# A hybrid of deformable convolution, attention and experts on one core: batch 0's samples by TensorE, sums sent by ScalarE, values copied by VectorE, fewer transfers of features, and one finishing job at a time in its heavy part

## The chip, the cores and the metric

The kernel runs on one core of a Trainium2 chip. The metric is the device time of one execution in microseconds. A core has five engines, each with an instruction order of its own: TensorE (PE in the profile; its weight loads are shown as PEld), VectorE (DVE), ScalarE (ACT), GpSimd (POOL) and SyncE (SP). "SPq", "ACTq" and "POOLq" are the same sequencers issuing transfers. Matmul results go to PSUM banks, from which VectorE or ScalarE copies them.

## The reference

The input x is [4, 128, 64, 64] in float32; a batch has 4096 positions, called tokens from the second layer on.

```python
# layer 0
g = groupnorm(x, 32 groups)
offset, mask = conv3x3(g), sigmoid(conv3x3(g))         # 18 and 9 channels
samples = bilinear_sample(g, grid + offset) * mask     # 9 taps of 128 channels a position
x = x + einsum("bckhw,ock->bohw", samples, w_flat) + bias
# layer 1, t = tokens of x, [4, 4096, 128]
n = layernorm(t)
c = cos(n.reshape(16 heads of 8) + theta)
q = [prod(c[1:]), c0*c1, c0*c1*c2, ...]                # 8 features of a head; q = k = v
ctx = softmax(q q^T / sqrt(8)) q                       # 4096 x 4096 for each head
x1 = layernorm(n + ctx @ w_comb.T + b_comb)
zf = cos(x1[..., :8]) * cos(ry)
t = t + layernorm(x1 + relu(zf @ w1.T + b1) @ w2.T + b2)
t = t + top2_of_8_experts(layernorm(t))                # router softmax, 8 matrices of 128 x 128
```

## The kernel before

A batch is cut into 8 chunks of 512 tokens, and the 16 heads into 4 groups of 4. The unit of attention is a step: for one run (a batch, a head group, a chunk of queries) and one tile of 128 keys, TensorE makes four score matmuls (L1261) into two PSUM tiles `sc`, ScalarE takes two exponentials of 128x1024 (L1270), and TensorE adds four context matmuls (L1281) to `acc`. There are 3700 steps. Where a chunk's exponentials are the mirror of a later one's, a few of them are turned by VectorE (`st`), sent to DRAM (`etd`) and read back (`et`) instead of being computed twice.

The order of TensorE, VectorE, SyncE and GpSimd is written out by hand: the main loop (from L1400 on) issues one step after another, and between steps a planner (`Beside`) places fills, pieces of the other work. The pieces come from Python generators that yield `need(pe, dve, lat, hold, after)`, an estimate of the piece's time; `Beside` keeps a planned clock that moves by 1.82 a step, a credit of TensorE time, and a list of things to do `later`, among them most transfers. Three kinds of job are queued:

- "prepare", for one batch: GroupNorm, a table of corner values in DRAM, offsets, then `deform`, which gathers samples, `convolved` (the conv of a chunk, the residual, the tokens) and `features`. Where a step needs a chunk that isn't there, the planner forces prepare work in front of it.
- "finish", for each chunk whose 4 head groups are done (`park_context`): `finish` loads the context, makes the reciprocals of the softmax sums and takes them through DRAM to spread them, then goes through `attention_out` (ao_ps), `feed_forward` (z_ps, h_ps, f_ps) and `experts` (u_ps, l_ps, e_ps, y_ps), and sends the output. At most two of the generators `finishing` are active at once, and each takes one chunk after another.
- "turned", for the mirrored exponentials.

After the last step `beside.drain()` writes out what finishing is left.

Batch 0 has nothing to hide its preparation behind, so its first 26 runs (steps 0 to 159, `opening`) work with the chunks that are there: chunk 1 is first needed at step 16, chunk 2 at 64, chunk 3 at 104, chunks 4 to 7 between 256 and 292. Such a run ends with a partial sum: ScalarE copies `acc` to `cu` (L1491), SyncE sends it to `part` (L1126) and loads it back for the run that goes on with it (L1456). Batch 1 begins at step 964, batch 2 at 1876, batch 3 at 2788; in batch 3 one chunk after another is done, the last with step 3700.

`deform` handles a chunk in 12 units of 128 positions by three taps: three indirect gathers on GpSimd (L625), a multiplication by the corner weights and two sums on VectorE (L645, L650, L651). For batch 0's chunks 0 and 1 the samples are then transposed on TensorE (L662) into PSUM and copied by VectorE into the tile `sT` of the conv. All other chunks use three VectorE transposes a unit (L686), four transfers to DRAM (`smd<-tr`, L698) and four back (`sT<-smd`) for each three taps of a chunk. Gathers run up to four units ahead for batch 0's first 36 units and two ahead otherwise.

`features` ends in `rn`: GpSimd copies it to `fx` (L823), four transfers write that to `fqd` (L827), TensorE transposes it (fT_ps, L836), VectorE splits the result into a high and a low part, and eight transfers (L846, L847) write each part twice to `kTd` (rows for keys) and twice to `qTd` (rows for queries).

Of the kernel before, what the change touches and what calls it, by code (L numbers as in the profile page):

```python
# [224 lines left out]
def kernel(  # L225
# [373 lines left out]
    def deform(b, tab, idx, wt, rest):  # L599
# [7 lines left out]

        def early(n):

            return b == 0 and n < 3 * 12  # L610

        def gather(last):

# [20 lines left out]
        for n, (ch, kg, j) in enumerate(units):  # L634
            progress[b] = 0.1 + 0.9 * n / len(units)
            if b == 0 and n == 36:
                yield need(dve=5.0)
                settle()
            while not ahead:
                yield need(lat=0.5)  # L640
            v, landed = ahead.pop(0)
            v4 = v.rearrange("p k (q c) -> p (k q) c", c=C)
            w12 = wt[:, j, 3 * kg : 3 * kg + 3, :].rearrange("p k q -> p (k q)")
            yield need(dve=ve(1536), after=landed)
            nc.vector.tensor_tensor(v4, v4, w12[:, :, None].to_broadcast([P, 12, C]), ALU.mult)  # L645
            if moved:
                yield need(pe=0.01, dve=ve(384))
                moved.pop()()
            yield need(dve=ve(768) + ve(384))
            nc.vector.tensor_tensor(v[:, :, : 2 * C], v[:, :, : 2 * C], v[:, :, 2 * C :], ALU.add)  # L650
            nc.vector.tensor_tensor(v[:, :, :C], v[:, :, :C], v[:, :, C : 2 * C], ALU.add)  # L651
            if b == 0 and ch < 2:


                if n % 12 == 0:
                    while len(summed) < ch:
                        yield need(lat=0.5)
                    sT = big.tile([P, KK, CH], F32, tag="xs", name=f"sT_first{ch}")
                yield need(pe=tr(3), lat=FREE, hold=True)
                pt = misc(f"sT_ps{j}_{kg}")  # L660
                for k in range(3):
                    nc.tensor.transpose(pt[:, P * k : P * (k + 1)], v[:, k, :C], ident)  # L662

                def move(sT=sT, kg=kg, i=j % 4, pt=pt):
                    nc.vector.tensor_copy(
                        sT[:, 3 * kg : 3 * kg + 3, P * i : P * (i + 1)],
                        pt[:, : 3 * P].rearrange("p (k c) -> p k c", c=P),
                    )

                moved.append(move)  # L670
                beside.later(beside.now + 0.8, lambda n=n: gather(n))
                if n % 12 == 11:
                    yield need(pe=0.01, dve=ve(384))
                    moved.pop()()
                    featuring.append(True)
                    beside.add("prepare", convolved(b, ch, sT), 0.5, True)
                    if ch == 0:
                        yield from rest
                continue

            yield need(dve=ve(384))
            if j % 4 == 0:
                beside.flush(sent)
                tr9 = work.tile([P, 4, 4, 4, 32], F32, tag="st", name=f"tr{b}_{ch}_{kg}", bufs=NST)
            for k in range(3):
                nc.vector.transpose(  # L686
                    out=tr9[:, k, :, j % 4, :],
                    in_=v[:, k, :C].rearrange("p (c i) -> p c i", i=32),
                )
            beside.later(beside.dve, lambda n=n: gather(n))  # L690
            if j % 4 < 3:
                continue
            while kg == 0 and len(featuring) > 1:
                yield need(lat=1.0)

            def put(ch=ch, kg=kg, tr9=tr9):
                for o in range(4):
                    nc.sync.dma_start(  # L698
                        out=smd[ch % 2][:, 3 * kg : 3 * kg + 3, :, o].rearrange(
                            "i k c n -> i (k c) n"  # L700
                        ),
                        in_=tr9[32 * o : 32 * (o + 1), :3].rearrange("p k c j t -> p (k c) (j t)"),
                    )

            sent = beside.dve
            beside.later(sent, put)
            if kg == 2:

                while len(summed) < ch if b == 0 else featuring:
                    yield need(lat=1.0)  # L710
                featuring.append(True)
                beside.later(
                    beside.dve + 0.1,
                    lambda ch=ch: beside.add("prepare", convolved(b, ch), 0.5, True),
                )
# [77 lines left out]
    def features(b, ch, x2, mean, rstd):  # L793

        yield from layer_norm_stats(x2, mean, rstd, "lt")

        def temp(name, shape=(P, 4 * C), dt=F32):
            return work.tile(list(shape), dt, tag="p2", name=f"{name}{b}_{ch}", bufs=NP2)

        fx, f4 = fxs[ch % NFX]  # L800
        xt, a, n, r = temp("xt"), temp("ra"), temp("rn"), temp("rr")
        yield need(dve=ve(128, 4))
        normalized(xt.rearrange("p (i c) -> p i c", c=C), x2, mean, rstd)
        beside.later(
            beside.dve,
            lambda: nc.sync.dma_start(out=xtd[b][ch].rearrange("p i c -> p (i c)"), in_=xt),
        )
        yield need(dve=ve(512, 2))
        a8 = a.rearrange("p (h d) -> p h d", d=HD)
        x8 = xt.rearrange("p (h d) -> p h d", d=HD)  # L810
        nc.vector.tensor_tensor(a8, x8, rx_sb[:, None, :].to_broadcast([P, 64, HD]), ALU.add)
        yield from cosine(a, a, n, r, ve(512))
        c8 = a.rearrange("p (j h d) -> p j h d", j=4, d=HD)
        q8 = n.rearrange("p (j h d) -> p j h d", j=4, d=HD)
        yield need(dve=ve(64, 7))
        nc.vector.tensor_tensor(q8[:, :, :, 0], c8[:, :, :, 1], c8[:, :, :, 2], ALU.mult)
        for d in range(3, HD):
            nc.vector.tensor_tensor(q8[:, :, :, 0], q8[:, :, :, 0], c8[:, :, :, d], ALU.mult)
        yield need(dve=ve(64, 7), lat=0.2)
        nc.vector.tensor_tensor(q8[:, :, :, 1], c8[:, :, :, 0], c8[:, :, :, 1], ALU.mult)  # L820
        for d in range(2, HD):
            nc.vector.tensor_tensor(q8[:, :, :, d], q8[:, :, :, d - 1], c8[:, :, :, d], ALU.mult)  # L822
        beside.later(beside.dve, lambda: nc.gpsimd.tensor_copy(f4[:, :, :, :HD], q8))  # L823

        def put_values():
            for g in range(NGRP):
                nc.sync.dma_start(out=fqd[b % 2][ch][g], in_=fx[:, :, QG * g : QG * g + QL])  # L827

        beside.later(beside.dve + 2.0, put_values)

        yield need(pe=tr(4), dve=ve(512, 2))
        pt = misc(f"fT_ps{b}_{ch}")
        for i in range(4):
            nc.tensor.transpose(pt[:, P * i : P * (i + 1)], n[:, P * i : P * (i + 1)], ident)  # L836
        hi, lo = temp("hiT"), temp("loT")
        nc.vector.tensor_copy(hi.bitcast(F32R), pt)
        nc.vector.tensor_tensor(lo.bitcast(F32R), pt, hi, ALU.subtract)

        def put(part, fT):

            kd = kTd[b % 2][ch].rearrange("(h l r d) n -> l r h d n", l=2, r=2, d=HD)
            qd = qTd[b % 2][ch].rearrange("(h r l d) n -> l r h d n", l=2, r=2, d=HD)
            for rep in range(2):
                nc.sync.dma_start(out=kd[part, rep], in_=fT)  # L846
                nc.sync.dma_start(out=qd[part, rep], in_=fT)  # L847

        beside.later(beside.dve - ve(512), lambda: put(0, hi))
        beside.later(beside.dve, lambda: put(1, lo))  # L850
        prepared[b, ch] = beside.dve + 9.0
        featuring.pop(0)

# [230 lines left out]
    def finish(b, ch):  # L1084
# [19 lines left out]
            in_=rdd[b][ch].rearrange("h q n -> h (q n)")[:, None, :].to_broadcast([HEADS, HD, CH]),  # L1104
        )
        yield from attention_out(b, ch, r, aT, a4)
        yield from feed_forward(b, ch, x4, a4)
        yield from experts(b, ch, x4)


    def park_context(b, g, sc, cu):
# [8 lines left out]

        beside.later(beside.dve, put)

    def park_sums(g, sc, cu, when):

        def put():
            nc.sync.dma_start(out=partd[g][sc], in_=cu)  # L1126
            storing.discard((g, sc))

        storing.add((g, sc))
        beside.later(when, put)  # L1130

# [90 lines left out]

    landing = {}
    fetched = {}
    groups, done, active = {}, [], []

    def finishing():

# [179 lines left out]
    with tc.manual_schedule(engines={PE, DVE, SP, POOL}):  # L1410
# [6 lines left out]
        while n < len(steps):  # L1417
# [71 lines left out]
                cu = work.tile([P, 512], F32, tag="cu", name=f"cu{run}", bufs=NCU)  # L1489
            if by_act:  # L1490
                nc.scalar.copy(cu, acc)  # L1491
            elif kind in (WHOLE, FIRST):
                nc.vector.tensor_copy(cu, acc)  # L1493
            else:
                nc.vector.tensor_tensor(cu, cu, acc, ALU.add)
            if kind in (WHOLE, LAST):
                park_context(b, g, sc, cu)
            else:
                park_sums(g, sc, cu, beside.now + 3.0 if by_act else beside.dve)
        alone.append(True)  # L1500
        beside.drain()

# [72 lines left out]
```

## Time and profile before

| | |
|---|---|
| median of 11 runs | 7461.57 us (7446.05 to 7471.73) |
| the profiled execution's own time | 7456.55 us |
| its span | 7454.8 us |
| ScalarE busy | 6853.9 us, of it 6839.9 in the 7400 exponentials |
| PE busy | 7028.4 us |
| VectorE busy | 4464.6 us |
| POOL busy | 1657.5 us |
| first exponential of the attention starts | 174.7 us |
| last exponential ends | 7370.9 us |

A line of the costliest groups reads: source line, engine, operation, output<-input, shapes, count | busy us, mean ns of one | idle us of the engine just before them, and what ended most of it. A line of the waits reads: engine, tile and line that waited <- who released it: us in total, times, longest us. The table of stretches gives, for start:end, the length and for each engine the busy us, then the granted TensorE clock as a share of full speed, the DMA engines' share and GB/s. A line of the timeline reads: start us, duration us, engine, line, operation, tile, count [idle us of the engine before it <- what ended it].

### The profile page before, as it was taken

The page shows a single profiled execution, that of the slowest core. Times are in us where ns is not written, and L with a number is a line of the kernel's source. Part 1 is how long each engine was busy: PE and PEld are TensorE (multiplying, and loading weights), DVE is VectorE, ACT ScalarE, POOL GpSimd, SP SyncE. Part 2 cuts the span into 40 slices and gives each one's busy share as a digit, 9 for nine tenths or more (in the row PEclk, how much of TensorE's full clock was granted, in tenths as well). Part 3 has the DMA queues.
Part 4 walks back from the last instruction along what each step waited for, and adds up shares of the span by engine and source line. Part 5 has one row for each costly group of instructions (what it writes and reads, how often), then busy time and mean ns, then how long its engine had stood idle before and what let it go on. Part 6 is the DMA issues. An engine that isn't in the chain of part 4 may idle for free.

```text
span 7454.8 us, 180754 instructions
## 1 busy us (share of the span) xinstructions
PE 7028.4 (94%) x73848; PEld 2360.6 (32%) x73848; DVE 4464.6 (60%) x8950; ACT 6853.9 (92%) x7467; POOL 1657.5 (22%) x1326
## 2 busy tenths in 40 slices
PE   3689999899999999999999999999999999999997
PEld 2222232223333333333333333323333333333333
DVE  7756366676445787875544778875444554455544
ACT  0579999899999999999999999989999999999995
POOL 5545034443001433431000434430000000000000
PEclk6889999999999999999999999999999999999998
DMA  6777567988446988887555888996454466666651
GB/s 182 223 210 230 139 233 241 304 257 289 152 162 229 297 261 273 288 277 235 201 180 193 268 287 293 315 313 226 172 180 150 158 233 232 239 223 229 231 196 64
DMA packets 909789, 1689.53 MB, mean 227 GB/s; under 512 B 150754, under 2 KB 384124, under 8 KB 858268
## 3 DMA queue, kind: packets, MB, share of 16 engines
q1 hardware_dynamic: 809102, 1371.37, 55.3%
q0 software_dynamic: 92160, 302.06, 12.5%
q8 instruction: 580, 9.50, 0.5%
q10 hardware_dynamic: 7694, 4.52, 0.2%
q14 instruction: 253, 2.07, 0.1%
HBM read 1027.51 MB, written 650.14 MB: 225 GB/s over the span
## 4 chain that ended last, share of the span: by engine, by line
PE 81%; DMA 9%; DVE 4%; SPq 1%; issue 1%; ACT 1%; POOL 0%; POOLq 0%; DVEq 0%; ACTq 0%
PE acc L1281 39%; PE sc L1261 23%; PE acc L1214 5%; PE conv_ps L281 4%; PE e_ps L281 4%; DMA et<-etd 3%; PE f_ps L281 2%; DMA etd<-st 1%; DMA sT<-smd 1%; PE om_ps L533 1%; DMA v<-tab,idx 1%; DMA smd<-tr 1%; ACT e L1270 1%; DVE v L645 1%; PE ao_ps L281 0%
## 5 line engine op out<-in xcount | busy, mean ns | idle before, releaser
L1270 ACT ACTIVATE e<-sc 128x1024 f32<-128x1024 f32 x7400 | 6839.9, 1084 | 411.3 <-PE sc L1261 332.4
L1281 PE MATMUL acc<-e,qf 128*9 128x512 f32 (+1 forms) x29600 | 3904.9, 600 | 11.3 <-ACT cu L1491 6.2
L1261 PE MATMUL sc<-qT,kT 32*128 32x512 f32 x14800 | 2326.1, 499 | 108.1 <-ACT e L1270 56.2
L1261 PEld LDWEIGHTS sc<-qT,kT 32*128 32x128 f32 x14800 | 929.2, 183 | 3528.3 <-ACT e L1270 3330.4
L625 POOL DMA_INDIRECT v<-tab,idx x1152 | 1457.4, 1265 | 1496.8 <-DVE tr L686 869.3
L1140 DVE STREAM_TRANSPOSE st<-e 128x1024 f32<-128x1024 f32 x792 | 937.1, 1221 | 709.1 <-ACT e L1270 586.3
L1281 PEld LDWEIGHTS acc<-e,qf 128*9 128x9 f32 (+1 forms) x29600 | 681.1, 92 | 577.7 <-issue 316.5
L396 POOL TENSOR_TENSOR r<-ln_t,expo 128x4 f32<-128x4 f32 x96 | 112.2, 1169 | 3095.7 <-DVE ln_t L394 3048.3
L645 DVE TENSOR_TENSOR v<-v,wt 128x1536 f32<-128x1536 f32 x384 | 667.0, 1737 | 126.1 <-DMA v<-tab,idx 123.7
L1214 PE MATMUL acc<-et,qv 128*9 128x128 f32 x12672 | 503.5, 277 | 65.6 <-DMA et<-etd 65.6
L1065 DVE TENSOR_TENSOR eo<-e_ps,gt 128x512 f32<-128x512 f32 x256 | 175.2, 686 | 536.6 <-PE e_ps L281 532.9
L650 DVE TENSOR_TENSOR v<-v 128x768 f32<-128x768 f32 x384 | 367.1, 956 | 10.1
L281 PE MATMUL conv_ps<-sT,wconv_sb 128*32 128x256 f32 x4320 | 351.0, 399 | 14.9 <-DMA sT<-smd 14.8
L1214 PEld LDWEIGHTS acc<-et,qv 128*9 128x9 f32 x12672 | 270.0, 91 | 264.5 <-issue 201.8
L686 DVE STREAM_TRANSPOSE tr<-v 128x128 f32<-128x128 f32 x1080 | 249.4, 282 | 49.1 <-DMA etd<-st 40.4
L1493 DVE COPY cu<-acc 128x512 f32<-128x512 f32 x116 | 80.2, 691 | 282.6 <-PE acc L1281 280.7
L651 DVE TENSOR_TENSOR v<-v 128x384 f32<-128x384 f32 x384 | 215.8, 562 | 13.3
L396 POOL TENSOR_TENSOR rstd<-lt_t,expo 128x4 f32<-128x4 f32 x32 | 56.5, 1766 | 545.2 <-DVE lt_t L394 509.6
L281 PE MATMUL f_ps<-w_sb,h 128*32 128x128 f32 x4096 | 164.8, 280 | 0.0
L950 DVE TENSOR_SCALAR h<-h_ps,b_sb 128x512 f32<-128x512 f32 x128 | 94.9, 743 | 99.5 <-PE h_ps L948 89.7
L823 POOL COPY fx<-rn 128x512 f32<-128x512 f32 x32 | 26.9, 839 | 522.5 <-DVE rn L822 319.1
L965 DVE TENSOR_TENSOR a<-a,f_ps 128x512 f32<-128x512 f32 x32 | 21.9, 686 | 195.7 <-PE f_ps L281 195.7
(227 smaller groups left out, 3164.5 us busy)
## 6 DMA issues: line engine op xcount, KB each, us to landing
etd<-st SPq DMA_DIRECT2D x396, 1024.0 KB
et<-etd SPq DMA_DIRECT2D x396, 1024.0 KB
kT<-kTd SPq DMA_DIRECT2D x372, 256.0 KB
smd<-tr SPq DMA_DIRECT2D x360, 192.0 KB
sT<-smd SPq DMA_DIRECT2D x360, 192.0 KB
qT<-qTd SPq DMA_DIRECT2D x166, 256.0 KB
atd<-cu SPq DMA_DIRECT2D x128, 256.0 KB
qf<-fqd SPq DMA_DIRECT2D x372, 72.0 KB
```

Source lines behind the costliest of these rows:

```text
L281: nc.tensor.matmul(dst[c : c + 32], lhsT=lhsT[:, c : c + 32], rhs=rhs, start=start, stop=stop)
L625: nc.gpsimd.indirect_dma_start(out=v[:, k, :], out_offset=None, in_=tab, in_offset=bass.IndirectOffsetOnAxis(ap=idx[:, j, kk : kk + 1], ax ...
L645: nc.vector.tensor_tensor(v4, v4, w12[:, :, None].to_broadcast([P, 12, C]), ALU.mult)
L650: nc.vector.tensor_tensor(v[:, :, : 2 * C], v[:, :, : 2 * C], v[:, :, 2 * C :], ALU.add)
L651: nc.vector.tensor_tensor(v[:, :, :C], v[:, :, :C], v[:, :, C : 2 * C], ALU.add)
L686: nc.vector.transpose(out=tr9[:, k, :, j % 4, :], in_=v[:, k, :C].rearrange("p (c i) -> p c i", i=32),)
L1065: nc.vector.tensor_tensor(ws[hf], pe.rearrange("p (e c) -> p e c", c=C), gt[:, i, 4 * hf : 4 * (hf + 1), None].to_broadcast([P, 4, C]), AL ...
L1140: nc.vector.transpose(out=st[:, :, 2 * pr : 2 * pr + 2, :].rearrange("p o h (q j) -> p o (h q) j", j=32), in_=es[pr].rearrange("p h (q o i ...
L1214: nc.tensor.matmul(acc[32 * h : 32 * h + QW, P * kt : P * (kt + 1)], lhsT=qv[:, at : at + QW], rhs=e[:, :, h, 32 * t : 32 * (t + 1)], star ...
L1261: nc.tensor.matmul(ps[i // 2][:, i % 2, :], lhsT=kT[h : h + 32, P * (t % 4) : P * (t % 4 + 1)], rhs=qT[h : h + 32, :], start=True, stop=True,)
L1270: nc.scalar.activation(e, ps[pr], AF.Exp, scale=1.0 / math.sqrt(HD))
L1281: nc.tensor.matmul(acc[32 * h : 32 * h + width, :], lhsT=flat[:, first : first + width], rhs=es[h // 2][:, h % 2, :], start=(t == ts[0]), ...
```

## The change

- `early` is true for all of batch 0: its gathers run up to four units ahead throughout, with the spare buffers that so far only the first 36 units used.
- All of batch 0's chunks take the way of chunks 0 and 1: transposes on TensorE, copies by VectorE into the one buffer tagged "xs". The first unit of a chunk waits until the conv of the chunk before is summed.
- In `features` VectorE copies `rn` to `fx`, behind the high and low parts. The rows of `kTd` and `qTd` stand in a new order, so that one transfer with a repeated source writes both copies of a part, and one transfer writes the values of all four groups, last: five transfers instead of twelve.
- In the first 26 runs ScalarE issues the transfer of a partial sum itself, in its own order behind the copy; `park_sums` keeps the other runs.
- `heavy` is a list that `finish` looks at behind `attention_out`: while another job is between there and the end of `experts`, it yields 1.0 of planned latency and looks again.

```diff
         def early(n):
-            return b == 0 and n < 3 * 12
+            return b == 0
...
-            if b == 0 and ch < 2:
+            if b == 0:
...
-        beside.later(beside.dve, lambda: nc.gpsimd.tensor_copy(f4[:, :, :, :HD], q8))
-        def put_values():
-            for g in range(NGRP):
-                nc.sync.dma_start(out=fqd[b % 2][ch][g], in_=fx[:, :, QG * g : QG * g + QL])
-        beside.later(beside.dve + 2.0, put_values)
-        yield need(pe=tr(4), dve=ve(512, 2))
+        yield need(pe=tr(4), dve=ve(512, 3))
...
         nc.vector.tensor_tensor(lo.bitcast(F32R), pt, hi, ALU.subtract)
+        nc.vector.tensor_copy(f4[:, :, :, :HD], q8)
         def put(part, fT):
-            kd = kTd[b % 2][ch].rearrange("(h l r d) n -> l r h d n", l=2, r=2, d=HD)
-            qd = qTd[b % 2][ch].rearrange("(h r l d) n -> l r h d n", l=2, r=2, d=HD)
-            for rep in range(2):
-                nc.sync.dma_start(out=kd[part, rep], in_=fT)
-                nc.sync.dma_start(out=qd[part, rep], in_=fT)
-        beside.later(beside.dve - ve(512), lambda: put(0, hi))
-        beside.later(beside.dve, lambda: put(1, lo))
+            kd = kTd[b % 2][ch].rearrange("(p l r) n -> l p r n", l=2, r=2)
+            qd = qTd[b % 2][ch].rearrange("(p r l) n -> l p r n", l=2, r=2)
+            twice = fT[:, None, :].to_broadcast([P, 2, CH])
+            nc.sync.dma_start(out=kd[part], in_=twice)
+            nc.sync.dma_start(out=qd[part], in_=twice)
+        def put_values():
+            nc.sync.dma_start(
+                out=fqd[b % 2][ch].rearrange("g p t x -> p t g x"),
+                in_=fx.rearrange("p t (g x) -> p t g x", g=NGRP),
+            )
+        beside.later(beside.dve - 2.0 * ve(512), lambda: put(0, hi))
+        beside.later(beside.dve - ve(512), lambda: put(1, lo))
+        beside.later(beside.dve, put_values)
...
         yield from attention_out(b, ch, r, aT, a4)
+        while heavy:
+            yield need(lat=1.0)
+        heavy.append(True)
         yield from feed_forward(b, ch, x4, a4)
         yield from experts(b, ch, x4)
+        heavy.pop()
...
-    def park_sums(g, sc, cu, when):
+    def park_sums(g, sc, cu):
...
-        beside.later(when, put)
+        beside.later(beside.dve, put)
...
             if by_act:
                 nc.scalar.copy(cu, acc)
+                nc.scalar.dma_start(out=partd[g][sc], in_=cu)
...
-            else:
-                park_sums(g, sc, cu, beside.now + 3.0 if by_act else beside.dve)
+            elif not by_act:
+                park_sums(g, sc, cu)
```

More of the change, by code (lines that the diff above doesn't have):

```diff
@@ L1226 @@
     fetched = {}
-    groups, done, active = {}, [], []
+    groups, done, active, heavy = {}, [], [], []
     def finishing():
```

## The prediction

> **What bounds the kernel now.** I read the page first (busy times, then the costliest groups), then the list of waits, then busy times by stretches, then the order of events in the stalls and at the end.
>
> ```profile
> PE 7028.4 (94%) x73848; PEld 2360.6 (32%) x73848; DVE 4464.6 (60%) x8950; ACT 6853.9 (92%) x7467; POOL 1657.5 (22%) x1326
> ...
> L1270 ACT ACTIVATE e<-sc 128x1024 f32<-128x1024 f32 x7400 | 6839.9, 1084 | 411.3 <-PE sc L1261 332.4
> ...
> L823 POOL COPY fx<-rn 128x512 f32<-128x512 f32 x32 | 26.9, 839 | 522.5 <-DVE rn L822 319.1
> ```
>
> The bound is ScalarE's 7400 exponentials, two a step. PE looks busier, but a matmul held up by ScalarE counts as busy; the list of waits settles it: PE's score weights wait 3330 us for exponentials, the exponentials 332 us for scores.
>
> ```profile
> PEld sc L1261 <- ACT e L1270: 3330.4, 4389, 6.3
> ...
> ACT e L1270 <- PE sc L1261: 332.4, 83, 120.2
> POOL fx L823 <- DVE rn L822: 319.1, 19, 24.5
> ```
>
> By stretches (busy us of each engine, granted TensorE clock, DMA share):
>
> ```profile
> core 0: us, PE busy (x) PEld busy (x) DVE busy (x) ACT busy (x) POOL busy (x), PEclk, DMA share, GB/s
> ...
> 224.00:274.00 50.00, 7.05 (x28) 2.59 (x28) 43.56 (x89) 5.61 (x6) 30.42 (x23) 0.50 0.72 226
> ...
> 474.00:524.00 50.00, 27.87 (x204) 8.67 (x204) 31.59 (x48) 19.43 (x21) 34.60 (x28) 0.63 1.02 287
> ...
> 5085.00:7371.00 2286.00, 2283.25 (x25734) 792.20 (x25734) 1092.57 (x2519) 2283.66 (x2495) 55.24 (x54) 1.00 0.58 200
> ...
> 7389.00:7455.00 66.00, 26.91 (x325) 15.85 (x325) 40.07 (x122) 0.23 (x1) 3.02 (x3) 0.60 0.01 5
> ```
>
> There are three regimes. In the opening ScalarE starves (5.61 busy of 50 us). From 5085 us to the last step it is busy 2283.66 of 2286 us, although finishing jobs run beside it: there they cost nothing. After the last step nothing covers them. ScalarE's order shows the largest stalls, before steps 16, 104 and 292:
>
> ```profile
> 267.94 2.85 ACT L1270 ACTIVATE e<-sc 128x1024 f32<-128x1024 f32 x3 [48.53 <-PE sc L1261]
> ```
> ```profile
> 487.00 5.61 ACT L1270 ACTIVATE e<-sc 128x1024 f32<-128x1024 f32 x6 [15.48 <-PE sc L1261]
> ```
> ```profile
> 885.39 3.77 ACT L1270 ACTIVATE e<-sc 128x1024 f32<-128x1024 f32 x4 [11.31 <-PE sc L1261]
> ```
>
> Events of the end:
>
> ```profile
> 7382.94 0.69 DVE L892 COPY y_6T<-y_ps 128x512 f32<-128x512 f32 x1 [0.56 <-PE y_ps L890]
> ...
> 7402.35 1.01 PE L939 MATMUL z_ps<-ident,zx 128*32 128x128 f32 x4 [10.43 <-DVE zx L935]
> ...
> 7450.44 0.69 DVE L892 COPY y_7T<-y_ps 128x512 f32<-128x512 f32 x1 [0.57 <-PE y_ps L890]
> 7451.16 0.34 SPq L1081 DMA_DIRECT2D out_dram<-y_7T  x1
> ```
>
> The exponentials end at 7370.9, the span at 7454.8: a tail of 83.9 us. A finishing job that runs alone takes 7450.44 − 7382.94 = **67.5 us** from one output copy to the next, and 48.1 us from its z_ps (start of feed_forward). After the copy come 4.4 us.
>
> **The gate (`heavy`): the largest term.** It adds no instruction; it changes the written order. Reading the order of PE's instructions in both programs, by attention steps (two score groups each): before, two finishing jobs interleave and y_ps of chunk 7 of batch 2 stands at step 3225 of 3700; after the last step remain chunk 7 and most of chunk 6's experts. In the changed program jobs stand one behind another, 84 steps apart (y_ps at 3279, 3363, 3447, 3531); batch 2's chunk 7 comes at 3531, and batch 3 has only chunks 0 and 1 done at 3697. Behind step 3700 stand chunk 2 from z_ps on and the whole of 4, 5, 6, 7 and 3; VectorE's order agrees, so engines can't overlap jobs more than the order lets them. Each job's loads stand ahead of the previous job's output copy, as in the row above, and 1/x with its DRAM round trip behind it, also as there. So the tail is 48.1 + 5 × 67.5 + 4.4 = 390 us, against 83.9: **+306**. What leaves the loop for this lay beside a ScalarE with 2 us idle in 2286, so the loop can't pay it back there. Bounds for one job: 40 us (VectorE's busy time alone) to 75 (loads from 7373 on exposed too): +148 to +343. I take 67.5, the same sequence alone.
>
> **Samples of batch 0.** Chunks 2 to 7 are 72 units. Each loses three VectorE transposes (282 ns, 0.85) and gains three on PE (0.88 by chunks 0 and 1) and a VectorE copy of 128x384 (0.55): VectorE −21 us, PE +63. 144 transfers of 192 KB leave SP's queue, four of which stand in front of the key loads of step 16. New: the copies go into a single buffer, so a chunk's first copy waits until the former chunk's conv is summed; and transposes wait in PE's queue, in order, for their gather, with scores behind them. At step 16 x_ps comes at step 12 instead of 16, without those four transfers (4.95 us) and a `pow` behind gathers (9.2): −18 (0 to −30). At step 64 the features of chunk 2 (fT_ps at step 47 before) are forced at the step that needs them: +19 by conv and features in a row (0 to 25). Chunk 3's are at step 88 instead of 100: the 15.5 goes. Late next is chunk 7, needed at 292: fT_ps stood at 282 and stands at 292 with the whole conv in front. In a row: last two units 4.4, conv 11 (351.0/32), x and LayerNorm 6.9, features 13.7, transposes and copy 1.4, writes and loads 18.3 (chunk 0: 155.6 to 173.9) = 55.7 against 11.3: +44 (+15 to +55).
>
> **Sums from ScalarE.** SP's 26 `part<-cu` (337 ns median) go. Reloads of sums ended ScalarE's idle times of 11.6, 6.7, 2.2, 12.6, 6.9 and 4.6 us in the opening, which is behind SP's queue: −44.5 if all go (0 if the reload's own round trip is what counts); I take all, with a shorter queue ahead. ScalarE, the bound, pays 26 issues; its own transfers at the start took 0.36 to 0.45 us: 26 × 0.42 = +11 (+9 to +26 with waits for a shared semaphore).
> The Trainium skill (DMA: Bandwidth & Descriptors, "Issuing engines are not separate DMA queues") speaks against this part: another issuing engine "will only save the time on the sequencer it takes to initiate the DMA". By it the saving is SP's 26 × 0.34 = 9 us, off the path, and the part is a loss of about 2 to 11 us; no run yet shows which.
>
> **Features.** POOL loses 32 copies of 839 ns and 319.1 us of waiting in order, which matters where gathers stand behind (only before 5150 us). VectorE gains 32 × 0.69 = 22 us over the loop, under ScalarE. SP loses 7 × 32 issues of about 0.6 us. Where a stall waits for features, chunk 0 shows eight writes issued over 155.67 to 162.4 and the next load at 169.47; the bytes stay the same: 0 (−4 to +2).
> The same page ("Anatomy of one DMA") puts some 2.0 us of fixed cost on a transfer; seven fewer would be 14 us a chunk, 42 over the three stalls. The row (eight issued within 6.8 us, landing together) doesn't show them one behind another, so the sum holds nothing of it.
>
> **Loop behind step 292.** 3408 steps took 6485.5 us; at 1.845 a step they need 6288, so some 195 us of idle can change, 77 of it at 885 to 1885 us, none behind 5085. Four finishing jobs fewer inside, one at a time: −20 (−80 to +40).
>
> **Sum.** Opening −18 + 19 − 15.5 − 44.5 + 11 + 44 = −4; loop −20; tail +306: +282. The profiled execution took 7456.55 (span 7454.8 and 1.75 around it), 5 us under the median: 7456.55 + 282 + 5 = 7743, told as **7740**. No measurement here tells under 0.2% (15 us) from nothing.
>
> **Rivals.** (a) Tail jobs overlap down to VectorE's 40 us: tail 5.7 × 40 + 4 = 232, +148; 7585. For it: 26 of 66 us of VectorE idle. Against: the order itself, and chunk 7 behind 6, which didn't overlap. (b) The opening gains nothing: reloads still wait, chunk 7's stall is longer, and loop stalls grow by 40: 7743 + 44.5 + 11 + 60 = 7860. For it: PE's in-order wait for gathers. (c) Faster: loop idle pays the tail. The loop can't be shorter than 174.7 + 3700 × 1.845 + 26 × 0.59 = 7017, 354 under 7370.9; if it all goes: 7461.57 + 306 − 354 = 7414. It decides from 306, 86% of all idle; against: 195 lies behind the opening, where little is changed. (d) The gate changes nothing at run time (jobs in pairs, tail 84): 7461.57 − 24 = 7438. Against: both orders.
>
> **Chances.** Forecast 0.83, (a) 0.06, (b) 0.07, (c) 0.02, (d) 0.02. Range: the bounds don't all fall together; opening (−57 to +67), loop (−80 to +40) and tail at 60 to 72 us a job (−40 to +25) give 7650 to 7830; (a), (c), (d) and the worst of (b) lie outside. Slower: 0.83 + 0.06 + 0.07 = 0.96; faster 0.03 with (c) and most of (d); same 0.01.
>
> **What would show it.** Right: last exponential 20 to 90 us earlier than 7370.9 or about there, then some 390 us with ScalarE idle, six y copies 67.5 apart; ScalarE's stall at step 16 near 30, a new one at 64, none at 104, near 55 at 292; L823 gone from POOL. Wrong: y copies about 40 apart (a); a tail near 84 (d); a loop over 300 us shorter (c).

## The result and the profile after

The changed kernel takes 7789.12 us (median of 8 runs, 7781.01 to 7806.04) against 7458.63 us of the kernel before (31 runs): 330 us more, a ratio of 1.0446 (95% interval 1.0437 to 1.0455). The forecast was 7740 us, with a range of 7650 to 7830. The result lies 49 us above the forecast; the loop is where it comes from, 54 us longer than told (table below).

The page of the changed kernel (busy times, the costliest group) and a line of its waits:

```profile
PE 7152.2 (92%) x74064; PEld 2420.1 (31%) x74064; DVE 4464.2 (57%) x8838; ACT 6848.1 (88%) x7467; POOL 1615.6 (21%) x1294
...
L1275 ACT ACTIVATE e<-sc 128x1024 f32<-128x1024 f32 x7400 | 6833.3, 1085 | 474.7 <-PE sc L1266 420.0
```
```profile
PEld sc L1266 <- ACT e L1275: 3308.9, 4462, 3.3
...
ACT e L1275 <- PE sc L1266: 420.0, 78, 120.1
```

ScalarE's work is the same (6848.1 us busy, 6853.9 before) and so is VectorE's (4464.2 and 4464.6); nothing has become slower to compute. What changed is when it is done. The stretches of the changed kernel:

```profile
core 0: us, PE busy (x) PEld busy (x) DVE busy (x) ACT busy (x) POOL busy (x), PEclk, DMA share, GB/s
...
224.00:274.00 50.00, 26.57 (x142) 9.69 (x146) 41.54 (x58) 17.25 (x19) 32.03 (x24) 0.60 0.72 231
...
474.00:524.00 50.00, 48.90 (x465) 15.37 (x461) 10.30 (x20) 46.83 (x52) 8.68 (x8) 0.97 0.34 109
824.00:874.00 50.00, 20.71 (x235) 8.97 (x233) 26.08 (x58) 9.56 (x11) 1.52 (x2) 0.74 0.23 74
5085.00:7397.00 2312.00, 2299.03 (x25247) 785.58 (x25239) 1056.58 (x2347) 2299.35 (x2513) 75.42 (x68) 1.00 0.59 204
```
```profile
7420.00:7786.00 366.00, 148.28 (x1769) 88.64 (x1769) 222.09 (x666) 1.37 (x6) 15.10 (x15) 0.61 0.06 17
```

In the opening ScalarE has more to do (17.25 of 50 us where it had 5.61, 46.83 where it had 19.43), but around 824 to 874 us it starves. Behind 7398 us it has next to nothing to do, for 392 us. ScalarE's order shows the stalls that are left, in front of steps 64 and 292:

```profile
376.41 3.77 ACT L1275 ACTIVATE e<-sc 128x1024 f32<-128x1024 f32 x4 [20.84 <-PE sc L1266]
```
```profile
877.69 2.86 ACT L1275 ACTIVATE e<-sc 128x1024 f32<-128x1024 f32 x3 [44.13 <-PE sc L1266]
```

In front of step 16 there are 31.1 us where there were 48.5, and the 15.5 us in front of step 104 are gone. The output copies of the tail:

```profile
7444.23 0.69 DVE L893 COPY y_2T<-y_ps 128x512 f32<-128x512 f32 x1 [0.57 <-PE y_ps L891]
...
7512.75 0.69 DVE L893 COPY y_4T<-y_ps 128x512 f32<-128x512 f32 x1 [0.57 <-PE y_ps L891]
...
7581.06 0.69 DVE L893 COPY y_5T<-y_ps 128x512 f32<-128x512 f32 x1 [0.57 <-PE y_ps L891]
...
7649.39 0.69 DVE L893 COPY y_6T<-y_ps 128x512 f32<-128x512 f32 x1 [0.57 <-PE y_ps L891]
```

They are 68.3 to 68.5 us apart, one finishing job behind another; y_7 follows at 7717.66 and y_3 at 7785.98. The 335.1 us by which the span grew (7789.9 − 7454.8) split at two moments of ScalarE's order, the first exponential of step 292 and the end of the last one:

| part | before | after | difference | forecast |
|---|---|---|---|---|
| start to step 292 | 885.4 | 877.7 | −7.7 | −4 |
| step 292 to the last exponential | 6485.5 | 6519.9 | +34.4 | −20 |
| tail | 83.9 | 392.3 | +308.4 | +306 |

### The profile page after: what moved, and what is told of

Same layout as the page of the kernel before. It is cut to its first block, busy times and chain, and to the rows that moved or that the text cites. A ratio compares the mean times of both kernels' runs of the same rounds, so it can differ in the third digit from the quotient of the medians.

```text
span 7789.9 us, 180503 instructions
## 1 busy us (share of the span) xinstructions
PE 7152.2 (92%) x74064; PEld 2420.1 (31%) x74064; DVE 4464.2 (57%) x8838; ACT 6848.1 (88%) x7467; POOL 1615.6 (21%) x1294
## 4 chain that ended last, share of the span: by engine, by line
PE 80%; DMA 8%; DVE 7%; SPq 1%; issue 1%; ACT 1%; POOL 0%; POOLq 0%; ACTq 0%; DVEq 0%
PE acc L1286 39%; PE sc L1266 23%; PE acc L1219 5%; PE conv_ps L281 3%; PE e_ps L281 3%; DMA et<-etd 3%; DMA sT<-smd 2%; PE f_ps L281 2%; ACT e L1275 1%; PE om_ps L533 1%; DMA rdd<-rd 1%; DVE v L645 1%; DVE st L1145 1%; PE ao_ps L281 1%; DMA etd<-st 1%
## 5 line engine op out<-in xcount | busy, mean ns | idle before, releaser
L1266 PE MATMUL sc<-qT,kT 32*128 32x512 f32 x14800 | 2365.0, 497 | 49.5 <-ACT e L1275 32.5
L1266 PEld LDWEIGHTS sc<-qT,kT 32*128 32x128 f32 x14800 | 949.8, 182 | 3489.8 <-ACT e L1275 3308.9
L1286 PEld LDWEIGHTS acc<-e,qf 128*9 128x9 f32 (+1 forms) x29600 | 665.3, 91 | 595.4 <-issue 346.0
L281 PE MATMUL conv_ps<-sT,wconv_sb 128*32 128x256 f32 x3456 | 281.7, 398 | 62.2 <-DMA sT<-smd 60.1
L686 DVE STREAM_TRANSPOSE tr<-v 128x128 f32<-128x128 f32 x864 | 199.2, 281 | 27.9 <-DMA etd<-st 19.0
L662 PE MATMUL sT_ps<-ident,v 128*128 128x128 f32 x288 | 63.0, 337 | 130.2 <-issue 109.6
```

The source lines that it names most:

```text
L281: nc.tensor.matmul(dst[c : c + 32], lhsT=lhsT[:, c : c + 32], rhs=rhs, start=start, stop=stop)
L686: nc.vector.transpose(out=tr9[:, k, :, j % 4, :], in_=v[:, k, :C].rearrange("p (c i) -> p c i", i=32),)
L1266: nc.tensor.matmul(ps[i // 2][:, i % 2, :], lhsT=kT[h : h + 32, P * (t % 4) : P * (t % 4 + 1)], rhs=qT[h : h + 32, :], start=True, stop=True,)
L1286: nc.tensor.matmul(acc[32 * h : 32 * h + width, :], lhsT=flat[:, first : first + width], rhs=es[h // 2][:, h % 2, :], start=(t == ts[0]), ...
```

## The experiments

They ran on three chips where the kernel before itself takes 7582 to 7601 us, so each is compared with the kernel before as timed beside it. The record doesn't name the chip of the first measurement, so that the chip makes the difference is not shown. The list of waits has more of PE's own issue there (`PEld sc <- issue` 446.2 us in the kernel before, 151.3 in its first profile) and 58.1 us in which exponentials wait for what the profile calls "remote" (another core or an unknown queue), 0 in the first; nothing shows why. "Loop" is step 292 to the last exponential in the profile, which is one execution; the kernel before, timed 19 times on one of these chips, spreads from 7562 to 7591 us, so a difference of a few microseconds between single profiles says nothing. On that footing the kernel before, run again as `before_here`, has step 160 at 637.5, step 292 at 903.6, a loop of 6592.8 and a tail of 85.6 us.

> The kernel before once more, for a profile beside the next three on the same chip: a tail near 84 us, and idle times of ScalarE at steps 16, 104 and 292 as in its first profile. If a chip only makes transfers slower, the stretches in which batches are prepared are longer than in the first profile and those behind step 2788 are not.

It came as expected for the most part: the stalls in front of steps 16, 104 and 292 are 41.2, 11.7 and 11.3 us (48.5, 15.5 and 11.3 before), the stretch behind step 2788 is as long as in the first profile (894.7 and 788.3 us to step 3273 and to the end, 894.7 and 788.2 before), the stretches with preparation are longer.

### The gate

Without it (the finishing jobs' pool then needs 12 buffers instead of 11, which alone leaves the order of the kernel before as it is):

```diff
-        while heavy:
-            yield need(lat=1.0)
-        heavy.append(True)
         yield from feed_forward(b, ch, x4, a4)
         yield from experts(b, ch, x4)
-        heavy.pop()
-NF2 = 11
+NF2 = 12
```

> The changed kernel without the gate, and with 12 instead of 11 buffers of the pool of the finishing jobs. In the written order chunk 6's last experts and chunk 7 stand behind the last step, as in the kernel before. My theory (the gate's order makes the tail): tail near 84 us instead of 392, so about 7790 - 308 = 7480 us if the 34 us that the loop behind step 292 lost come from another part, and about 7450 if they come from the gate. Rival (the gate is innocent, some other part of the change keeps finishing back): near 7780.

Measured: 7684.27 against 7600.68 us, ratio 1.0114 (1.0096 to 1.0132). The tail is 82.8 us (7682.5 − 7599.7): the long tail is the gate's. But the kernel is still 84 us slower than before, more than either forecast.

The gate alone, in the kernel before:

```diff
         yield from attention_out(b, ch, r, aT, a4)
+        while heavy:
+            yield need(lat=1.0)
+        heavy.append(True)
         yield from feed_forward(b, ch, x4, a4)
         yield from experts(b, ch, x4)
+        heavy.pop()
```

> The kernel before with the gate as its only edit. Behind the last step stand the rest of chunk 2's experts and the whole of chunks 4, 5, 6, 7 and 3. My theory: tail 20 + 5 x 68.3 + 4.4 = 366 us, loop as before (ends near 7371): 7740 us; 7770 if the gate also costs the loop its 34 us. Rival (the gate needs another part of the change to do harm): near 7460.

Measured: 7937.06 against 7600.68 us, ratio 1.0439 (1.0416 to 1.0463), as much as the whole change. VectorE's order at its end:

```profile
7604.65 0.69 DVE L892 COPY y_2T<-y_ps 128x512 f32<-128x512 f32 x1 [0.57 <-PE y_ps L890]
...
7672.18 0.69 DVE L892 COPY y_4T<-y_ps 128x512 f32<-128x512 f32 x1 [0.57 <-PE y_ps L890]
```

The last exponential ends at 7596.1, chunk 2's copy follows 8.5 us later, and then come jobs 67.5 to 68.1 us apart, the last one (chunk 3) 54.1; the tail is 338.0 us, 252 more than `before_here`'s, and 28 less than I expected, for these two reasons (8.5 instead of 20, 54.1 instead of 68.3). The other 84 of the 336 us are in the loop, where I had allowed the gate 34 at most.

A smaller dose, the gate around `experts` alone (`alone` is set behind the last step, so that the gate is open there):

```diff
         yield from attention_out(b, ch, r, aT, a4)
-        while heavy:
+        yield from feed_forward(b, ch, x4, a4)
+        while heavy and not alone:
             yield need(lat=1.0)
         heavy.append(True)
-        yield from feed_forward(b, ch, x4, a4)
         yield from experts(b, ch, x4)
-        heavy.pop()
+        heavy and heavy.pop()
```

> The changed kernel with the gate around experts alone (opened behind the last step). A smaller dose: behind the last step stand chunk 5 from z_ps on (48 us), the whole of chunks 6 and 7 and the rest of chunk 4's experts (30 to 40). My theory: tail 48 + 2 x 68.3 + 35 + 4.4 = 224 us, about 7620 us (7590 if the loop's loss shrinks with the gate). Rival (the tail is set by something else than the number of jobs left): 7450 or 7790.

Measured: 7828.68 us, ratio 1.0297 (1.0276 to 1.0319); the tail is 251.1 us, with copies 68.4 and 68.3 us apart. Four output copies (chunks 5, 6, 7 and 4) stand behind the last step instead of six, and the tail is 141 us shorter than the changed kernel's, two jobs' time: its length goes with the number of jobs left. It is 27 us longer than expected, since chunk 5's copy comes 71.7 us behind the last exponential and not 48. The gate is open in this tail, and the copies stand as far apart as behind a closed one: without another order, jobs still follow one another.

Whether the jobs could have overlapped, had the order let them:

```diff
             job = left[0] if left[0]["need"][3] is None else self.lock or left[0]
+            if name is None:
+                self.turn += 1
+                job = left[self.turn % len(left)]
+                if job["need"][0] and self.lock is not None:
+                    job = self.lock
             self._run(job)
...
-        while heavy:
+        while heavy and not alone:
...
-        heavy.pop()
+        heavy and heavy.pop()
```

> The changed kernel with its gate up to the last step; behind it the gate is open and the finishing jobs are written out two at a time, a piece of one and a piece of the other in turn (12 buffers instead of 11). Same loop and same 5.7 jobs in the tail. If only the written order keeps jobs apart (the reason why rival (a) was given little), the period of a job falls from 68.3 to between 40 (VectorE's busy time) and 50 us: tail 230 to 290 us, 7630 to 7690 us. If the engines can't do better than one job behind the other, the tail stays at 392 and the time at 7790.

Measured: 7878.96 us, ratio 1.0364 (1.0342 to 1.0385), tail 292.0 us. The pairs in VectorE's order:

```profile
7671.12 0.68 DVE L899 COPY y_2T<-y_ps 128x512 f32<-128x512 f32 x1
7682.50 0.66 DVE L899 COPY y_3T<-y_ps 128x512 f32<-128x512 f32 x1
```
```profile
7771.03 0.68 DVE L899 COPY y_4T<-y_ps 128x512 f32<-128x512 f32 x1
7782.37 0.66 DVE L899 COPY y_5T<-y_ps 128x512 f32<-128x512 f32 x1
```

Two jobs take 99.9 us, 50 each instead of 68.3; VectorE's own 40 is not reached. So 100 us of the tail were due to the serial order; the engines would have allowed it. Rival (a)'s 40 us a job is a bound that even this order doesn't reach, and the serial order was the reason why it didn't happen.

All four runs are slower than expected by their ratios too: taken to the first measurement's 7458.63 us, they stand for 7544 (`no_gate`), 7786 (`gate_alone`), 7680 (`gate_experts`) and 7730 us (`tail_pairs`), 16 to 64 us above the highest time that my theory gave each. In the profiles their loops lose far more than the 34 us of the first comparison (see the loop, below).

### The parts of the opening

All three start from `no_gate` (step 160 at 603.9, step 292 at 904.4, loop 6695.3) and undo one part.

```diff
         def early(n):
-            return b == 0
+            return b == 0 and n < 3 * 12
...
-            if b == 0:
+            if b == 0 and ch < 2:
```

> The changed kernel without the gate (12 buffers), and batch 0's chunks 2 to 7 again by VectorE transposes and DRAM. By the prediction's terms (step 16 -18, step 64 +19, step 104 -15.5, step 292 +44) the samples part costs 30 us up to step 292: this kernel should start step 292 about 30 us earlier than no_gate, with a stall near 11 there. Rival (the gain at 16 and 104 is the sums' or the features', not the samples'): earlier by 60. The loop behind step 292 as in no_gate if its loss isn't from this part.

Measured: 7607.03 against 7581.66 us, ratio 1.0035 (1.0025 to 1.0046); step 160 at 638.6, step 292 at 903.3. Undoing the samples part gives back all that steps 16 to 160 had won, 35 us, with the reload waits back (11.0, 6.8, 8.3, 10.6 and 7.1 us). It brings nothing at step 292, since the 44 us in front of it shrink to 12.9 at the same time. The loop is 6622.4 us, 73 us shorter than `no_gate`'s; 54, if the 19 us by which the kernel before differed between the two comparisons are taken off. So some of the loop's loss goes with the samples part.

```diff
             if by_act:
                 nc.scalar.copy(cu, acc)
-                nc.scalar.dma_start(out=partd[g][sc], in_=cu)
...
-            elif not by_act:
-                park_sums(g, sc, cu)
+            else:
+                park_sums(g, sc, cu, beside.now + 3.0 if by_act else beside.dve)
```

> The changed kernel without the gate (12 buffers), with SyncE sending the sums. By the prediction's terms ScalarE's issues win 44.5 us of reload stalls and cost 11: this kernel should start step 292 about 33 us later than no_gate. Rival (the reloads wait because SyncE's queue is full of sample transfers, so the samples part alone removes those stalls): about 11 us earlier than no_gate.

Measured: 7656.86 us, ratio 1.0094 (1.0065 to 1.0123); step 160 at 605.0, step 292 at 910.3. Sending the sums from ScalarE is worth 1 us at step 160 and 6 at 292, not 33; single profiles on two chips don't tell that from nothing. The rival was nearer: the reload waits go with the samples' transfers. ScalarE's idle time in front of its copies of sums, steps 16 to 160, was 49.8 us before and 18.3 in the changed kernel; it is 20.4 here, with SyncE sending, and 51.3 in `old_samples`, where ScalarE sends but the samples go through DRAM. SyncE's order in the kernel before shows what a reload (`cu<-part`) stood behind, ahead of the 11.6 us stall at 276.3:

```profile
268.82 1.04 SPq L698 DMA_DIRECT2D smd<-tr  x1
269.91 1.70 SPq L722 DMA_DIRECT2D xr<-in_x_dram  x1
271.70 5.47 SPq L731 DMA_DIRECT2D sT<-smd  x8
277.51 0.34 SPq L1456 DMA_DIRECT2D cu<-part  x1
```

PE uses this reload from 285.8 us on, 8 us after its issue. In the changed kernel the first reload is issued at 246.6, 16 us ahead of its use, and PE doesn't wait for it.

But ScalarE doesn't pay 11 us either, as the rival had it. In the changed kernel its issue lies inside an exponential that is already running:

```profile
263.76 0.59 ACT L1496 COPY cu<-acc 128x512 f32<-128x512 f32 x1 [3.16 <-PE acc L281]
264.25 1.03 ACT L1275 ACTIVATE e<-sc 128x1024 f32<-128x1024 f32 x1
264.38 0.33 ACTq L1497 DMA_DIRECT2D part<-cu  x1
265.16 4.70 ACT L1275 ACTIVATE e<-sc 128x1024 f32<-128x1024 f32 x5
```

The issue at 264.38 takes 0.33 us, and the next exponential follows the running one without a gap. So it is with 22 of the 26 issues of the changed kernel; the other four stand in idle times of ScalarE (31.1, 20.8, 1.5 and 0.4 us).

```diff
-            twice = fT[:, None, :].to_broadcast([P, 2, CH])
-            nc.sync.dma_start(out=kd[part], in_=twice)
-            nc.sync.dma_start(out=qd[part], in_=twice)
+            for rep in range(2):
+                nc.sync.dma_start(out=kd[part, rep], in_=fT)
+                nc.sync.dma_start(out=qd[part, rep], in_=fT)
...
-        nc.vector.tensor_copy(f4[:, :, :, :HD], q8)
+        beside.later(beside.dve, lambda: nc.gpsimd.tensor_copy(f4[:, :, :, :HD], q8))
```

(with the old row order and the four transfers of values)

> The changed kernel without the gate (12 buffers), with GpSimd's copy and 12 transfers a chunk. By the prediction's terms the features part is worth nothing at the stalls (0, -4 to +2): steps 0 to 292 within 5 us of no_gate. If the loop's loss behind step 292 comes from this part (larger transfers in front of loads, the copy on VectorE), the loop behind 292 is 30 us or more shorter than no_gate's; if it comes from the order in which the planner happens to place fills, it moves by some 20 us either way, without a pattern by batch.

Measured: 7605.08 us, ratio 1.0033 (1.0022 to 1.0043); step 292 at 899.3, the loop 6620.9 us. Twelve transfers instead of five cost nothing in front of the stalls (step 292 comes 5 us earlier). Behind them the loop is 74 us shorter than `no_gate`'s, 55 with the 19 us taken off: as much of the loop's loss goes with the features part as with the samples.

### The loop

The features part alone, in the kernel before (its diff is that of the change; 12 buffers):

> The kernel before with the features part as its only edit (and 12 buffers, which leave the order of the kernel before as it is). If fewer and larger transfers with the values last cost the loop, the loop behind step 292 is 25 us or more longer than before's on the same chip; if that loss is one of placement (what the planner puts in front of which landing transfer), it lies within 25 us of before, to either side. Up to step 292 within 6 us of before in any case.

Measured: 7608.61 against 7583.15 us, ratio 1.0034 (1.0021 to 1.0046); step 292 at 901.1, loop 6630.5, 38 us longer than `before_here`'s.

An edit that changes no work, behind the opening:

```diff
                 if run == opening:
                     beside.rate = beside.RATE
+                if run > opening and run % 8 == 5:
+                    beside.dve = max(beside.dve, beside.now + 3.0)
```

> The kernel before with an edit that changes no work: behind the opening, in each eighth run, the planner takes VectorE to be busy 3 us longer than it plans, so that fills stand a little elsewhere. If placement alone moves the loop (PE held in order by a transfer that lands later than planned), the loop behind step 292 changes by 15 us or more; if placement matters little and the losses belong to the parts of the change, it stays within 10 us of before.

Measured: ratio 1.0000 (0.9990 to 1.0009), loop 6597.9, 5 us longer. The theory that the loop moves with any small shift of the fills falls for this shift, the only one tried; that leaves the parts as the likelier cause of the loop's losses.

### Towards a faster kernel

```diff
         def early(n):
-            return b == 0 and n < 3 * 12
+            return b == 0 and n < 5 * 12
...
-            if b == 0 and ch < 2:
+            if b == 0 and ch < 4:
```

> The kernel before with one edit: chunks 2 and 3 of batch 0 also go by TensorE, and gathers run four ahead for the first 60 units; chunks 4 to 7 stay with VectorE and DRAM. No gate, old features, sums by SyncE, 11 buffers. In the changed kernel steps 16 to 160 came 33 us early and a row of chunk 7's conv and features in front of step 292 took it back. In this order fT_ps of chunk 3 stands at step 92 (100 before) and of chunk 7 at 275 (282 before). My theory: 25 to 35 us early at step 160, a stall of 11 or less at 292, so some 30 us early there; behind it the loop as before within 20 us; ratio 0.993 to 0.999. Rival (the gain of the opening needs the other parts): no earlier than before.

Measured: 7584.76 against 7583.15 us, ratio 1.0000 (0.9992 to 1.0009). The stall in front of step 292 is gone and the step comes 17 us early (886.2), but step 160 does not (636.3): there eight loads of samples that still go through DRAM stand in front of the reloads again (issued from 572.4 to 581.2, the reloads at 582.4 and 587.3, a 10.4 us wait from 587.2). In the profile the 17 us at step 292 are there, with a loop 7 us longer than `before_here`'s (span 7569.9 against 7582.0), but that execution is 13 us under the median of its kernel; the timing doesn't tell the kernel from before.

The same with the tail of `tail_pairs` and 12 buffers:

> samples_2_3 (chunks 2 and 3 of batch 0 by TensorE, no gate, all else as before) with the tail of tail_pairs: behind the last step the rest of chunk 6 and chunk 7 are written out in turn, 12 buffers. In tail_pairs that took a job's period from 68 to 51 us; here only the end of one job lies beside the start of the other, so that chunk 7's reciprocals and their DRAM round trip (6 us) and its ao_ps part begin beside chunk 6's experts: tail 84 to 68-78 us, with the opening's 17 us early at step 292: ratio 0.997 to 0.999. If VectorE, waiting in order for the load of the sums, holds up chunk 6's experts by as much, the tail stays near 84 and the ratio at 1.000.

Measured: 7576.89 against 7582.69 us, ratio 0.9996 (0.9987 to 1.0005). The tail is 82.2 us, 84 in `samples_2_3`. VectorE's order behind the last exponential (7497.3) shows the miss:

```profile
7498.42 0.69 DVE L1499 COPY cu<-acc 128x512 f32<-128x512 f32 x1
7504.75 0.55 DVE L1103 RECIPROCAL rd<-rd 128x64 f32<-128x64 f32 x1 [5.64 <-DMA rd<-atd]
```

The reciprocals now stand in front of the rest of chunk 6's experts and wait 5.64 us for the load of the sums, and everything behind them on VectorE waits too. With more of chunk 7's work written between, chunk 6's output copy comes 31.8 us behind the last exponential, against 12.0 in `samples_2_3`; chunk 7's then follows after 46.5 us instead of 68.0. What the second job gains the first one loses. That is the case the expectation named, of which the reciprocals' wait is a part; no version here beats the kernel before by more than can be told.

## Why the prediction was right, and where it was off

**The gate, +306: right, +308.4.** The mechanism was as read: the jobs left behind the last step come one behind another, 68.3 us from copy to copy where 67.5 was told, and don't overlap. `gate_alone` shows the cause (tail 338.0 us with that one edit), `no_gate` that nothing else makes the tail (82.8), `gate_experts` that it goes with the number of jobs. VectorE is busy 222.09 of 366 us in the tail, so 144 us of it are waits within one job; `tail_pairs` makes the tail 100 us shorter by putting two jobs beside each other.

**The opening, −4: right in sum (−7.7), wrong in two of its terms; that they cancel is luck.**
- Step 16, −18: right, −18.3 (249.6 against 267.9).
- Step 64, a new stall of some 19 us: right, 20.8. Step 104, −15.5: right, no stall.
- Step 292, +44: mis-sized. The stall is 44.1 us, not 55.7, so it costs +32.8 (44.1 − 11.3). The work stood in a row as told, but 12 us shorter: writes and loads took 11.2 us (865.6 to 876.8), not the 18.3 of chunk 0; the conv 8.0, not 11; the last units 2.9, not 4.4; features 12.4, not 13.7; transposes and copy 1.9, not 1.4. From step 160 to 292 the changed kernel still lost 42.7 us, since some 9 us of small waits came in that no term held.
- "Sums from ScalarE", −44.5 and +11: this step failed in both numbers. The reloads waited behind the samples' transfers in SyncE's order, so their end belongs to the samples part (35 us at step 160 by `old_samples`). They didn't all go either: idle time in front of the copies fell by 31.5 us (49.8 to 18.3). And an issue under a running exponential cost ScalarE nothing. The part is worth 1 to 6 us (`sums_by_sp`), if anything. The samples part was booked at −14.5 up to step 160 and the sums at −33.5; measured together they came to −50.4.

The prediction weighed against this part the sentence of the Trainium skill (DMA: Bandwidth & Descriptors, "Issuing engines are not separate DMA queues") that another issuing engine only saves the sequencer's time. The runs side with it on the saving: small, 1 to 6 us. What an issue costs the bound engine the lines at 264 us show: about nothing.

**Features, 0 in front of the stalls: right.** Step 292 moved by 5 us in `old_features` and 2.5 in `features_alone`, and the stall in front of it is 44.8 us with twelve transfers (`old_features`) and 44.5 with five (`no_gate`).
The same page puts a fixed cost of some 2.0 us on a transfer ("Anatomy of one DMA — SWDGE (gpsimd) path", so for those that GpSimd issues; these are SyncE's); the prediction's estimate from it, 14 us a chunk for seven transfers fewer, shows in none of these runs.

**Loop behind step 292, −20: failed, +34.4.** I argued that fewer finishing jobs inside the loop must leave fewer stalls. There were more: ScalarE's idle from step 292 on rose from 189 to 230 us. On PE the time stands in waits for samples on their way to a conv:

```profile
PE conv_ps L281 <- DMA sT<-smd: 60.1, 13, 13.1
```

Before, that wait came to 14.8 us in 5 times:

```profile
PE conv_ps L281 <- DMA sT<-smd: 14.8, 5, 5.3
```

PE is in order, so scores stand behind it. The longest of these waits can be followed through SyncE's, PE's and ScalarE's orders in the changed kernel:

```profile
2733.30 3.55 SPq L844 DMA_DIRECT2D fqd<-fx  x1
2736.90 8.84 SPq L722 DMA_DIRECT2D xr<-in_x_dram  x1
...
2748.16 9.30 SPq L731 DMA_DIRECT2D sT<-smd  x4
...
2762.41 1.08 PE L281 MATMUL conv_ps<-sT,wconv_sb 128*32 128x256 f32 x8 [13.06 <-DMA sT<-smd]
...
2766.02 4.75 ACT L1275 ACTIVATE e<-sc 128x1024 f32<-128x1024 f32 x5 [14.55 <-PE sc L1266]
```

Behind the features' five transfers the issue of `xr` takes 8.84 us, the loads of samples are issued late, the conv waits 13.06 us for them and ScalarE 14.55 us for the scores behind the conv. The longer issue comes with the features part: between 885 and 5100 us `xr<-in_x_dram` takes 2.5 us on average in the changed kernel and 2.2 in `features_alone`, 0.8 before and 0.9 in `old_features`.

The experiments put the loss on the parts rather than on chance. Against `before_here` (one profile each) the loop is 38 us longer with the features alone, 28 with samples and sums (`old_features`), 30 with features and sums (`old_samples`), 77 with samples and features (`sums_by_sp`), and, with the 19 us between the chips taken off, some 83 for all three (`no_gate`) and for the gate alone. These don't add up: with the gate as well, `tail_pairs` loses some 63, and the changed kernel itself, whose order up to the last step is the same, lost 34 in the first comparison. That the gate costs the loop anything is the plainest contradiction of the step: jobs one at a time were meant to relieve it.

What stays open is the rest of the mechanism. The chain above is shown for the changed kernel only; in `features_alone` PE waits just 6.2 us for `sT<-smd`, though the loop loses 38 us, and nothing shows how the gate alone loses its 83. For these I can say which parts lose the time, not how.

**Rivals.** (a), overlapping jobs, did not happen, for the reason given. (b) came true in half: the loop lost 34 us (40 in the rival), the opening did not lose. (c) and (d) fell: the loop had nothing to give back, and the gate acts at run time as it stands in the order.

## What to carry to other kernels

Work that runs free beside a bound engine isn't free when it's late: count, in the order of the built program, what stands behind the bound engine's last instruction, and price it by the same work measured alone, job after job. A limit on how many background jobs run at once is a limit on their throughput; compare it with the rate at which they arrive. And when a term says that a wait ends, find the transfers that stand in front of it in the issuing queue before choosing which part of a change gets the credit: here one part's gain was booked on another, and the sum was right by luck.

## What the runs showed of the hardware

- A transfer issued by ScalarE while its activation runs (0.33 us within 1.03 us) delayed no later activation; 22 of the 26 in the changed kernel stand so, and all together cost the bound engine nothing that step 160 shows (603.9 us with them in `no_gate`, 605.0 without in `sums_by_sp`).
- Fewer and larger transfers in a row don't free SyncE by as much as their number falls: the five took 4.6 us of issue a chunk instead of 9.3 for twelve (885 to 5100 us), but `xr<-in_x_dram`, often the next issue, went from 0.8 to 2.5 us on average.
- The same program took 7459 us in the first measurement and 7582 to 7601 on the three chips of the experiments; in the two profiles the difference lies before step 2788 (5688.0 us to there, 5813.3 in `before_here`) and none of it behind. Only comparisons of runs timed beside each other carry a per cent here.
